# Two small copies of a state-space layer moved from compute engines to DMA, in a kernel whose instruction order is planned at build time

## The chip, the cores and the metric

The kernel runs on one core of one Trainium2 chip. The metric is the device time of one execution in microseconds (us), the median of several runs. Engine names are those of the profile: PE is TensorE's matmul, PEld its weight load, DVE is VectorE, ACT is ScalarE, POOL is GpSimd, and SP is SyncE, which in this kernel only issues DMAs.

## The reference, cut to what matters

Two layers act on `x` of shape 2 x 2048 x 256. Each layer normalises its input, computes a branch `s` and a gate `g`, and adds `s * silu(g)`. In the first layer `s` is a Mamba block and `g` an FFN with blockwise FP4 quantisation; in the second layer `s` is a small attention (its softmax runs over the batch of two) and `g` three blocks of a quantised linear pair with LoRA. The change concerns the Mamba block:

```python
xi, z = jnp.split(x @ in_proj_w, 2, axis=-1)             # 512 channels each
xc = lax.conv_general_dilated(xi, conv_w, padding=[(3, 0)], ...)   # causal, 4 taps, per channel
xc = silu(xc + conv_b)
dt, Bm, Cm = jnp.split(xc @ x_proj_w, [16, 32], axis=-1)
dt = softplus(dt @ dt_proj_w + dt_proj_b)
def step(h, inp):                                        # one time step, h: 512 channels x 16 states
    h = exp(dt_t * A) * h + dt_t * B_t * x_t
    y = sum(h * C_t, axis=-1)
    return h, y
_, ys = lax.scan(step, h0, xs)                           # 2048 steps, batch 2
y = (ys + D * xc) * silu(z);  s = y @ out_proj_w
```

Two things are carried along the sequence: the last three columns of `xi`, which the causal convolution needs, and the state `h`.

## The kernel before

**Chunks.** The sequence is cut into 8 chunks of T = 256 steps, for each of two batch rows b. The order is (j, b) with j outermost, so there are 16 chunk steps; the chunk of (j, b) needs what (j-1, b) left two steps earlier. A chunk step has four parts: `head` (normalise, in-projection, convolution, `dt`, `B`, `C`), `fp4_half`, `scan` and `tail`. After both batch rows of a j, `second` computes the second layer for two groups of 128 steps.

**The convolution.** `xi` is a tile of 128 partitions x 4 channel groups x (3 + 256) columns with one buffer. ACT fills columns 3 and on from PSUM; columns 0 to 2 are the history, from a small constant tile `hist[b]`. After ACT's copies the last three columns go back to `hist[b]`. In the kernel before both moves are DVE copies of 128 x 12 elements. PE multiplies `xi` with diagonal matrices `cdiag`, 16 products of 256 columns to a bank.

**The recurrence.** `scan` takes the 16 states in 8 pairs, so there are 128 pairs in all. For each pair: a DMA brings B and C, broadcast to all partitions, into `bcs` (two buffers); ACT writes eight pieces of `decay = exp(dt * A)`; DVE writes `ux * B` into `hh` columns 1 to 256 (call it the product with B); column 0 of each of the 8 rows of `hh`, the seed, is the carried state from `state[b]`; one DVE scan runs over all 8 rows, 2056 elements; a DMA saves the last column to `state[b]`; DVE multiplies by C, shifted one column; PE transposes 16 blocks into the accumulating banks `y`. The tile `hh` has two buffers, so the seed and the product with B of pair k need the transposes of pair k-2 done. At j = 0 the seed is a memset on POOL (16 pairs); in the other 112 pairs it is an ACT copy of 128 x 8 elements.

**The order of the work.** Nothing is issued as it is written. `Recorder` records each call, with its stage (chunk step, part); `prepare` finds what depends on what; `forward` plays the program on a small model of the engines, whose durations come from `cost`, picking at each free engine the call of highest key; `backward` does the same from the end and gives new keys. `order` alternates both, once for each entry of the list `passes` (18 of them here, with hand-set offsets for a stage, or for a stage on one engine). `issue` then emits the calls in the order found, all of them on one line, so that in the profile nearly every instruction stands at L579 and is told by its tiles. Each engine and SP's queue execute in that order; buffers of each tile are handed out by the same plan. DMAs have a cost in the model of 0.52 us on SP, a tail of 1.7 us and 165e3 bytes per us.

Of the kernel before, what the change touches and what calls it, by code (L numbers as in the profile page):

```python
# [12 lines left out]
ALU = mybir.AluOpType  # L13
# [9 lines left out]
T = 256  # L23
# [18 lines left out]
class Recorder:  # L42
# [69 lines left out]
    def cost(self, engine, method, args, kwargs):  # L112
        out = kwargs.get("out", args[0] if args else None)
        n = 1
        for d in out.shape[1:]:
            n *= d
        if engine == "sync":
            return 0.52
        if engine == "gpsimd":
            if method == "memset":  # L120
                return 0.04
            return 0.69 if method == "tensor_tensor" else 0.19
        values = list(args[1:]) + list(kwargs.values())
        tiles = [v for v in values if hasattr(v, "tensor") and v is not out]
        if engine == "tensor":
            rhs = args[2] if len(args) > 2 else kwargs.get("rhs")
            if method == "transpose" or kwargs.get("is_transpose"):
                return 0.109
            if rhs.dtype == BF16:
                return 0.005 + n / 2400.0  # L130
            lhs = kwargs.get("lhsT", args[1] if len(args) > 1 else None)
            if lhs.shape[0] == 16 and lhs.offset >= 16 * lhs.ap[0][0]:
                return 0.1
            return 0.005 + 4 * max(n, 192) / 2400.0
        scalars = 0
        for v in tiles:
            m = 1
            for d in v.shape[1:]:
                m *= d
            scalars += m == 1 and n > 1  # L140
        if engine == "scalar":
            inside = bool(tiles) and self.space(tiles[0].tensor) == PSUM
            scalars += 1.5 * (kwargs.get("accum_out") is not None)
            return (0.05 if inside else 0.093) + 0.000833 * n + 0.1 * scalars
        if method == "tensor_tensor_scan":
            return 0.068 + 0.002083 * n
        if method == "bn_stats":
            return 0.333
        if method == "bn_aggr":
            return 0.1  # L150
        if method == "reciprocal":
            return 0.06 + 0.0066 * n
        if method == "tensor_reduce":
            n = 1
            for d in args[1].shape[1:]:
                n *= d
        if method in ("tensor_copy", "tensor_scalar", "memset") and n >= 64:
            if tiles and self.space(tiles[0].tensor) == PSUM:
                return 0.067 + 0.0010417 * n + 0.06 * scalars
            return 0.07 + 0.00052 * n + 0.06 * scalars  # L160
        if n <= 32:
            return 0.078
        return 0.067 + 0.0010417 * n + (0.06 if method == "scalar_tensor_tensor" and scalars else 0.0)
# [419 lines left out]
def tile_two_layers(ctx: ExitStack, tc: tile.TileContext, a: dict):  # L583
    nc = tc.nc
    rec = Recorder(nc, ctx.enter_context(tc.tile_pool(name="shadow", bufs=1, space=DRAM)))
# [124 lines left out]
    hist = [const.tile([P, 4, 3], F32, tag=f"hist{b}", name=f"hist{b}") for b in range(B)]  # L710
# [5 lines left out]
    state = [const.tile([P, NS, 4], F32, tag=f"state{b}", name=f"state{b}") for b in range(B)]  # L716
# [184 lines left out]
    def head(b, j, xt):  # L901
        nm = f"{b}_{j}"
        xn = io.tile([P, TG, D], F32, tag="xn", name=f"xn_{nm}", bufs=2)
        xh = t2k("m", f"xh_{nm}").rearrange("p (g d) -> p g d", g=TG)


        mv = statistics("m", xt, TG, f"x{nm}")
        rr = inverse_root("m", mv[:, :, 1], TG, 1.0 + EPS, EPS * EPS, f"a{nm}", (1.0, EPS))
        rh, rx = rr[:, :TG], rr[:, TG:]
        normalize("m", xh, xt, TG, mv, rh, f"a{nm}")  # L910
        normalize("m", xn, xt, TG, mv, rx, f"x{nm}")
        pt = transpose_pair("m", xh, f"a{nm}")
        lnt = mam.tile([P, 2, T], F32, tag="lnt", name=f"lnt_{nm}")
        for c in range(2):
            rec.scalar.activation(
                lnt[:, c, :], pt[:, c, :], AF.Identity,
                bias=ln1b[:, c : c + 1], scale=ln1g[:, c : c + 1],
            )
        xi = mam.tile([P, 4, T + 3], F32, tag="xi", name=f"xi_{nm}", bufs=1)
        if j == 0:  # L920
            rec.vector.memset(xi[:, :, 0:3], 0.0)
        else:
            rec.vector.tensor_copy(xi[:, :, 0:3], hist[b])
        for pr in range(2):
            px = bank("m", f"px_{nm}_{pr}").rearrange("p (m t) -> p m t", m=2)
            for mm in range(2):
                m = 2 * pr + mm
                for c in range(2):
                    rec.tensor.matmul(
                        px[:, mm, :], lhsT=w_in[:, c, m * P : (m + 1) * P], rhs=lnt[:, c, :],  # L930
                        start=(c == 0), stop=(c == 1),
                    )
            rec.scalar.copy(xi[:, 2 * pr : 2 * pr + 2, 3:], px)
        if j < NJ - 1:
            rec.vector.tensor_copy(hist[b], xi[:, :, T : T + 3])
        xc = mam.tile([P, 4, T], F32, tag="xc", name=f"xc_{nm}", bufs=1)
        for pr in range(2):
            pc = bank("m", f"pc_{nm}_{pr}").rearrange("p (m t) -> p m t", m=2)
            for mm in range(2):
                m = 2 * pr + mm  # L940
                for k in range(4):
                    rec.tensor.matmul(
                        pc[:, mm, :], lhsT=cdiag[:, m, k, :], rhs=xi[:, m, k : k + T],
                        start=(k == 0), stop=(k == 3),
                    )
            for mm in range(2):
                m = 2 * pr + mm
                rec.scalar.activation(xc[:, m, :], pc[:, mm, :], AF.Silu, bias=conv_b[:, m : m + 1])
        pd = bank("m", f"pxp_{nm}")
        for m in range(4):  # L950
            rec.tensor.matmul(
                pd[: 4 * R, :T], lhsT=w_xp[:, m].rearrange("p a b r -> p (a b r)"), rhs=xc[:, m, :],
                start=(m == 0), stop=(m == 3),
            )
        xdbl = mam.tile([4 * R, T], F32, tag="xdbl", name=f"xdbl_{nm}", bufs=1)
        rec.scalar.copy(xdbl, pd[: 4 * R, :T])
        bc = dram.tile([2 * NS, T], F32, tag="bc", name=f"bc_{nm}")
        for q in range(2):
            rec.sync.dma_start(bc[q * NS : (q + 1) * NS, :], xdbl[(2 * q + 1) * R : (2 * q + 2) * R, :])
        dt = mam.tile([P, 4, T], F32, tag="dt", name=f"dt_{nm}")  # L960
        ux = mam.tile([P, 4, T], F32, tag="ux", name=f"ux_{nm}", bufs=1)
        pdt = [
            bank("m", f"pdt_{nm}_{pr}").rearrange("p (m t) -> p m t", m=2)[:, :, :T]
            for pr in range(2)
        ]
        for mm in range(2):
            for pr in range(2):
                rec.tensor.matmul(
                    pdt[pr][:, mm, :], lhsT=w_dt[32 * pr : 32 * pr + R, mm * P : (mm + 1) * P],
                    rhs=xdbl[32 * pr : 32 * pr + R, :], start=True, stop=True,  # L970
                )
        for m in range(4):
            rec.scalar.activation(
                dt[:, m, :], pdt[m // 2][:, m % 2, :], AF.Softplus, bias=dt_b[:, m : m + 1]
            )
        rec.vector.tensor_tensor(ux, dt, xc, ALU.mult)
        return dict(xt=xt, xn=xn, lnt=lnt, xc=xc, dt=dt, ux=ux, bc=bc)

    def scan(b, j, h):
# [11 lines left out]
        for n in range(0, NS, 2):  # L991
# [14 lines left out]
            if j == 0:  # L1006
                rec.gpsimd.memset(hh[:, :, :, 0], 0.0)
            else:
                rec.scalar.copy(hh[:, :, :, 0], state[b][:, n : n + 2, :])
            rec.vector.tensor_tensor(hh[:, :, :, 1:], un, bn, ALU.mult)  # L1010
            flat = hh.rearrange("p k m t -> p (k m t)")
            rec.vector.tensor_tensor_scan(
# [294 lines left out]
    for i, (j, b) in enumerate(order):  # L1307
# [48 lines left out]
        (80, 1, 0.1, 0.3, 0.08, [(1, 0, -0.16), (12, 4, -0.06)]),  # L1356
        (50, 0.1, 0.1, 0.2, 0.08, []),
        (30, 0.5, 0.05, 0.567, 0.05, [(0, 1, 0.179), (1, 2, 'gpsimd', 0.202), (10, 1, 'vector', 0.118), (10, 4, 0.653), (11, 4, 'tensor', -0.045), (13, 3, 'tensor', 0.2), (14, 0, -0.07), (15, 2, 'gpsimd', -0.336), (4, 4, 'vector', 0.127), (5, 0, 0.109), (8, 4, 1.201), (9, 1, 'gpsimd', -0.424)]),
        (80, 1, 0.02, 1, 0.05, []),
        (20, 1, 0.1, 2, 0.02, []),  # L1360
        (20, 0.5, 0.1, 0.5, 0.12, [(11, 3, 'tensor', 0.138), (3, 0, 'tensor', -0.771), (5, 0, 'scalar', 0.427)]),
        (80, 0.1, 0.05, 2, 0.08, []),
        (20, 1, 0.1, 0.5, 0.12, []),
    ]
    rec.issue(tc, lead=(12.22, -6.26, 0, -7.42, 1.15), bonus=193.318, ahead=0.034, adjust=adjust, passes=passes)

# [47 lines left out]
```

## Time and profile before

| | |
|---|---|
| time, median of 3 runs | 1745.32 us (1740.76 to 1745.61) |
| the profiled execution | 1740.26 us, span 1738.5 us |
| granted TensorE clock, mean | 0.962 |
| busy, share of the span: DVE | 1629.0 us, 94% |
| PE | 1554.3 us, 89% |
| ACT | 1472.7 us, 85% |
| POOL | 180.2 us, 10% |
| DMA, share of 16 engines | 21.3%, 179358 packets |

The page gives busy time for each engine, then 40 slices of the span with a digit for each (9 is 90% or more), the DMA queues, the chain of work that ended last, and the costliest groups of instructions: engine, operation, output tile `<-` input tiles, shapes, count, busy time, mean of one, and the idle time of that engine just before them with what ended it. The chain starts from the last instruction and steps back to what released each one.

Three rows bear on the change. The ACT copies of the seed are 112 of 204 ns mean, 22.8 us in all. The two DVE copies of the history are 14 each, of 155 and 164 ns, 2.2 and 2.3 us. The DMA that saves the state, 112 times 4 KB, takes 606 ns of SP to issue and lands 2.3 us after its issue (median).

### The profile page before, as it was taken

The page shows a single profiled execution, that of the slowest core. Times are in us where ns is not written, and L with a number is a line of the kernel's source. Part 1 is how long each engine was busy: PE and PEld are TensorE (multiplying, and loading weights), DVE is VectorE, ACT ScalarE, POOL GpSimd, SP SyncE. Part 2 cuts the span into 40 slices and gives each one's busy share as a digit, 9 for nine tenths or more (in the row PEclk, how much of TensorE's full clock was granted, in tenths as well). Part 3 has the DMA queues.
Part 4 walks back from the last instruction along what each step waited for, and adds up shares of the span by engine and source line. Part 5 has one row for each costly group of instructions (what it writes and reads, how often), then busy time and mean ns, then how long its engine had stood idle before and what let it go on. Part 6 is the DMA issues. An engine that isn't in the chain of part 4 may idle for free.

```text
span 1738.5 us, 22023 instructions
## 1 busy us (share of the span) xinstructions
PE 1554.3 (89%) x7948; PEld 1224.5 (70%) x7948; DVE 1629.0 (94%) x1658; ACT 1472.7 (85%) x2903; POOL 180.2 (10%) x122
## 2 busy tenths in 40 slices
PE   7546978899899999989998999999899989997996
PEld 5335757687686868678785777787676767776765
DVE  8999999999999999999999999999999999999623
ACT  6546877779899999989998989999999998999443
POOL 0000100111110111100101002110202011200000
PEclk9768989999999999999999999999999999999999
DMA  7322121212212222222222221222122121111000
GB/s 182 94 57 49 39 55 44 49 40 55 42 50 62 37 52 48 56 43 50 50 50 62 48 45 46 54 43 56 38 49 50 44 56 43 50 43 50 6 6 13
DMA packets 179467, 87.23 MB, mean 50 GB/s; under 512 B 131575, under 2 KB 145565, under 8 KB 179358
## 3 DMA queue, kind: packets, MB, share of 16 engines
q1 hardware_dynamic: 179358, 85.83, 21.3%
q8 instruction: 62, 1.02, 0.2%
q14 instruction: 47, 0.39, 0.1%
HBM read 80.62 MB, written 4.72 MB: 49 GB/s over the span
## 4 chain that ended last, share of the span: by engine, by line
PE 28%; DVE 19%; ACT 11%; issue 6%; POOL 0%; ACTq 0%; DVEq 0%
DVE hh L579 13%; PE bank_f L579 11%; PE bank_m L579 6%; PE bank_s L579 5%; PE bank_y L579 4%; ACT L579 4%; ACT decay L579 3%; ACT t2k_s L579 2%; PE bank_h L579 2%; DVE fp_l L579 2%; DVE fp_sc L579 1%; DVE t2k_s L579 1%; ACT t2k_f L579 1%; DVE h L579 1%; ACT dt L579 0%
## 5 line engine op out<-in xcount | busy, mean ns | idle before, releaser
L579 DVE TENSOR_TENSOR_SCAN hh<-decay,hh 128x2056 f32<-128x2056 f32 x128 | 567.3, 4432 | 4.0 <-ACT decay L579 1.9
L579 ACT ACT_TABLE_LOAD x364 | 467.0, 1283 | 22.0 <-DVE hh L579 8.2
L579 ACT ACTIVATE decay<-dt,amat 128x256 f32<-128x256 f32 x1024 | 443.4, 501 | 48.8 <-DVE hh L579 47.2
L579 PE MATMUL bank_y<-ident,hh 128*128 128x128 f32 x2048 | 280.3, 283 | 48.1 <-DVE hh L579 43.4
L579 PEld LDWEIGHTS bank_y<-ident,hh 128*128 128x128 f32 x2048 | 246.1, 146 | 86.8 <-issue 43.8
L579 DVE TENSOR_TENSOR hh<-ux,bcs 128x2048 f32<-128x2048 f32 x128 | 291.7, 2279 | 2.9 <-PE bank_y L579 2.7
L579 DVE TENSOR_TENSOR hh<-hh,bcs 128x2048 f32<-128x2048 f32 x128 | 292.0, 2282 | 0.4
L579 POOL TENSOR_TENSOR ln_sq_s<-ln_sq_s,power 128x2 f32<-128x2 f32 x42 | 73.1, 1741 | 713.6 <-ACT ln_sq_s L579 713.6
L579 PE MATMUL bank_f<-w_f,t2k_f 128*128 128x256 f32 x512 | 129.6, 384 | 6.8 <-ACT t2k_f L579 6.7
L579 PE MATMUL bank_f<-t2k_f,w_f 128*128 128x256 f32 x512 | 122.9, 381 | 1.4 <-ACT t2k_f L579 1.1
L579 PE MATMUL bank_m<-xi,cdiag 128*128 128x256 f32 x512 | 123.5, 379 | 0.7 <-ACT xi L579 0.7
L579 PEld LDWEIGHTS bank_f<-w_f,t2k_f 128*128 128x128 f32 x512 | 93.2, 191 | 25.5 <-ACT t2k_f L579 11.7
L579 PEld LDWEIGHTS bank_f<-t2k_f,w_f 128*128 128x128 f32 x512 | 95.3, 190 | 18.1 <-ACT t2k_f L579 3.7
L579 PEld LDWEIGHTS bank_m<-xi,cdiag 128*128 128x128 f32 x512 | 94.4, 190 | 15.5 <-ACT xi L579 1.1
L579 PE MATMUL bank_f<-w_down,hq 128*128 128x256 f32 x384 | 97.7, 393 | 4.7 <-ACT hq L579 4.6
L579 PE MATMUL bank_h<-t2k_s,w_l 128*128 128x256 f32 x360 | 88.6, 385 | 9.9 <-ACT t2k_s L579 9.9
L579 DVE SCALAR_TENSOR_TENSOR fp_l<-fp_h,fp_l 128x704 f32<-128x704 f32 (+2 forms) x124 | 91.5, 738 | 5.2 <-ACT fp_h L579 4.6
L579 PE MATMUL bank_f<-w_gate,t2k_f 128*128 128x352 f32 x256 | 91.7, 479 | 4.9 <-ACT t2k_f L579 3.1
L579 PE MATMUL bank_f<-w_up,t2k_f 128*128 128x352 f32 x256 | 90.0, 468 | 6.7 <-DVE h L579 3.7
L579 PEld LDWEIGHTS bank_f<-w_down,hq 128*128 128x128 f32 x384 | 73.3, 197 | 22.5 <-ACT hq L579 8.7
L579 PE MATMUL bank_s<-w_qkv,t2k_s 128*128 128x256 f32 (+1 forms) x280 | 83.8, 432 | 4.0 <-DVE t2k_s L579 4.0
L579 PE MATMUL bank_s<-w_l,t2k_s 128*128 128x256 f32 x336 | 82.6, 384 | 4.5 <-ACT t2k_s L579 4.5
(191 smaller groups left out, 2454.5 us busy)
## 6 DMA issues: line engine op xcount, KB each, us to landing
bcs<-bc SPq DMA_DIRECT2D x128, 512.0 KB, 4.8
xt<-in_x_dram SPq DMA_DIRECT2D x16, 256.0 KB, 3.8
out_dram<-t2k_s SPq DMA_DIRECT2D x15, 256.0 KB, 2.2
w_f<-in_ffn_w_dram SPq DMA_DIRECT2D x2, 1024.0 KB, 9.7
state<-hh SPq DMA_DIRECT2D x112, 4.0 KB, 2.3
t2k_s<-in_qweights_dram SPq DMA_DIRECT2D x6, 256.0 KB, 5.9
w_in<-in_in_proj_w_dram SPq DMA_DIRECT2D x1, 1024.0 KB, 5.4
h<-in_w_gate_dram SPq DMA_DIRECT2D x6, 128.0 KB, 2.2
```

The source lines that it names most:

```text
L579: getattr(getattr(self.nc, engine), method)(*args, **kwargs)
```

## The change

The seed of `hh` is brought by a DMA on SP's queue instead of an ACT copy; the history is written and read back by DMAs on SP's queue instead of DVE copies. In the cost model a power on POOL is priced by its number of columns and another two-operand call there at 0.5. The last five entries of `passes` are replaced by nine others, so that the order of all instructions and the buffers are found anew; the first thirteen entries, `lead`, `bonus`, `ahead` and `adjust` stay.

```diff
         if engine == "gpsimd":
             if method == "memset":
                 return 0.04
-            return 0.69 if method == "tensor_tensor" else 0.19
+            if args[-1] == ALU.pow:
+                return 0.39 + 0.155 * n
+            return 0.5 if method == "tensor_tensor" else 0.19
...
-            rec.vector.tensor_copy(xi[:, :, 0:3], hist[b])
+            rec.sync.dma_start(xi[:, :, 0:3], hist[b])
...
-            rec.vector.tensor_copy(hist[b], xi[:, :, T : T + 3])
+            rec.sync.dma_start(hist[b], xi[:, :, T : T + 3])
...
-                rec.scalar.copy(hh[:, :, :, 0], state[b][:, n : n + 2, :])
+                rec.sync.dma_start(hh[:, :, :, 0], state[b][:, n : n + 2, :])
...
-        (80, 1, 0.02, 1, 0.05, []),
-        (20, 1, 0.1, 2, 0.02, []),
-        (20, 0.5, 0.1, 0.5, 0.12, [(11, 3, 'tensor', 0.138), (3, 0, 'tensor', -0.771), (5, 0, 'scalar', 0.427)]),
-        (80, 0.1, 0.05, 2, 0.08, []),
-        (20, 1, 0.1, 0.5, 0.12, []),
+        (110, 1, 0.02, 0.5, 0.05, [(11, 0, 0.05), (8, 2, -0.05)]),
+        (50, 0.3, 0.02, 1, 0.08, [(0, 4, -0.29)]),
+        (110, 0.3, 0.02, 0.2, 0.05, []),
+        (20, 1, 0.1, 1, 0.08, [(3, 0, -0.05)]),
+        (50, 1, 0.02, 2, 0.12, [(0, 2, -0.2)]),
+        (80, 0.5, 0.0, 0.2, 0.02, []),
+        (80, 0.5, 0.02, 0.3, 0.05, [(9, 0, 0.1)]),
+        (110, 1, 0.0, 0.2, 0.08, [(2, 2, 0.02)]),
+        (20, 0.1, 0.1, 0.5, 0.05, [(11, 2, 'gpsimd', 1.321), (13, 3, 'vector', -0.068), (8, 0, 'gpsimd', -0.605)]),
```

Counted from the two programs: DMAs on SP go from 381 to 521 (112 seeds, 14 histories out and 14 in); ACT's copies from 350 to 238 and its table loads from 364 to 351; DVE's copies from 37 to 9. Instructions that only wait go from 55 to 142 on PE, from 350 to 372 on DVE, from 272 to 367 on SP and from 331 to 266 on ACT. Every other kind of instruction has the same count.

## The prediction

> **What bounds the kernel now.** I read the page first (busy shares, slices), then stretches of the span, then who waits for whom on DVE, then the timeline around single pairs and the chain of waits near the end. The page:
>
> ```profile
> DVE  8999999999999999999999999999999999999623
> ACT  6546877779899999989998989999999998999443
> ```
>
> The stretches (columns after the length: PE, PEld, DVE, ACT, POOL busy, then clock, DMA share, GB/s):
>
> ```profile
> 200.00:400.00 200.00, 173.15 (x868) 136.56 (x867) 197.98 (x177) 157.54 (x300) 16.45 (x9) 0.94 0.21 48
> ...
> 1000.00:1200.00 200.00, 192.96 (x1014) 155.77 (x1012) 196.49 (x191) 187.96 (x369) 22.99 (x13) 0.99 0.21 46
> 1200.00:1400.00 200.00, 186.08 (x978) 146.50 (x978) 192.89 (x181) 190.33 (x373) 26.00 (x13) 1.00 0.22 49
> ...
> 1600.00:1671.00 71.00, 66.49 (x312) 51.89 (x310) 37.42 (x53) 39.28 (x83) 3.31 (x4) 0.95 0.05 11
> 1671.00:1738.40 67.40, 50.64 (x222) 37.55 (x222) 27.09 (x76) 22.59 (x40) 5.59 (x8) 0.91 0.04 12
> ```
>
> From 200 to 1600 us the seven stretches hold 1375.2 us of DVE in 1400: 24.8 us of idle time there, and 10.6 before 200. PE and ACT follow at 93 to 96%, so DVE sets the pace, with little room under either neighbour. After the last scan (it ends at 1613.7) DVE is mostly idle: to 1671 PE is at 94% and the chain of waits runs almost wholly through it; after that come the dependent steps of the second layer. Three limits, then: DVE's sum to about 1600, PE's queue to 1671, a chain to the end.
>
> What DVE waits for from 200 to 1600 (us in total, times, longest):
>
> ```profile
> DVE t2k_s L579 <- PE bank_s L579: 4.6, 4, 2.4
> DVE hh L579 <- PE bank_y L579: 2.7, 3, 1.6
> ...
> DVE hh L579 <- ACT decay L579: 1.9, 2, 1.2
> ```
>
> No wait is large. Little is to be won in this stretch, much could be lost.
>
> **The change part by part.** Durations are from the profiled execution, which took 1740.26 us (span 1738.5, 1.8 outside it). It stands 5.1 under the median of 1745.32 and at the lower end of the runs.
>
> *DVE copies.* 28 go, 155 and 164 ns, together 4.5 us. They overlap their neighbours: the one at 28.18 us of the timeline is followed by the next DVE start at 28.26, 0.08 us on, so 2.2 to 4.5; I take 3, on the saturated engine.
>
> *ACT copies and table loads.*
>
> ```profile
> L579 ACT COPY hh<-state 128x8 f32<-128x8 f32 x112 | 22.8, 204 | 7.4 <-PE bank_y L579 5.6 <-DVE hh L579 1.8
> L579 ACT ACT_TABLE_LOAD x364 | 467.0, 1283 | 22.0 <-DVE hh L579 8.2 <-PE bank_f L579 3.8 <-PE bank_h L579 1.7
> ```
>
> 112 copies give 22.8 us back, and ACT no longer stands in its queue for the transposes (5.6). The new order has 13 table loads fewer, 13 x 1.283 = 16.7. The Trainium skill (ScalarE: Activation LUTs, What ACT_TABLE_LOAD costs) prices a switch at 2.66 us, since a drain of 1.38 comes with the load; that would be 34.6. The trace shows no such drain: a load from 1590.46 for 1.28 us is followed by its ACTIVATE at 1591.76. So 16.7, and 39.5 in all. This lies beside DVE: ACT feeds it late only for a few us. What a lighter ACT can bring is a part of the 24.8 us of DVE idle, directly or through PE, which waits for ACT in turn; bounds 0 and 15, I take 5 (about the waits on ACT and POOL plus a share of those on PE).
>
> *The seed as a DMA.* No row shows a DMA into `hh`; the nearest is the same 1024 elements the other way:
>
> ```profile
> bcs<-bc SPq DMA_DIRECT2D x128, 512.0 KB, 4.8
> ...
> state<-hh SPq DMA_DIRECT2D x112, 4.0 KB, 2.3
> ```
>
> The skill speaks against this (DMA: Bandwidth & Descriptors, Rules for kernel authors): under 64 KB one pays mostly overhead, and a strided last dimension costs a descriptor for each element, as here, against a copy of 0.2 us. Taken on the path, 112 x 2.3 = 258 us. But the same table says to issue early and wait late, and the trace decides by the room there is. The seed may start when the transposes of pair k-2 end and must be there when scan k starts. A tight case:
>
> ```profile
> 1188.55 0.27 PE L579 MATMUL bank_y<-ident,hh 128*128 128x128 f32 x1
> 1188.86 2.29 DVE L579 TENSOR_TENSOR hh<-ux,bcs 128x2048 f32<-128x2048 f32 x1 [0.47 <-PE bank_y L579]
> 1190.82 0.20 ACT L579 COPY hh<-state 128x8 f32<-128x8 f32 x1
> 1191.26 4.44 DVE L579 TENSOR_TENSOR_SCAN hh<-decay,hh 128x2056 f32<-128x2056 f32 x1
> ```
>
> The last transpose ends at 1188.82, the scan starts at 1191.26: 2.4 us, because DVE does its product first. The same difference over all 112 pairs has a median of 8.2 us; 10 are below 3.0, 12 below 4, 25 below 5, 35 below 5.8. A seed that needs 2.9 (0.6 of issue, 2.3; counting the issue twice at worst) would lack 2.6 us in total in the old order, one that needs 4 would lack 14. SP's queue adds its own order. In the new program I traced, for each seed, what SP must have seen before it gets there: always the transposes of k-2 (once k-3), and a DVE instruction after which DVE still has, at the rows' durations, 11.9 us of work (median) before the scan; the smallest is 2.2, the next 3.5. `bcs`, queued behind seeds that wait for PE, keeps at least 4.6 (median 10.6) against 4.8 + 0.4 needed, because what blocks it is usually the transposes of the pair three before. So +1 us, bounds 0 and 14.
>
> *The histories.* 28 DMAs; the first convolution product waits for one. `xi<-hist` starts when the previous convolution frees `xi`, and the in-projection (8 products of 0.43) and ACT's `xi` copies (0.59) come in the same interval. The cover is the eight scans of the current chunk, some 95 us, beside which the next `head` runs. 0; if the cover were gone, 14 x 2.9 = 41 for PE, of which DVE would see what it waits for at `ux`.
>
> *SP, PE and DVE's waits.* SP issues 112 x 0.61 + 28 x about 0.5 = 82 us more; it waits 747 us for DVE's `hh` today. PE gets 87 more waiting instructions; at the 0.04 us that the chain shows as "issue" between dependent steps that is 3.5 us on an engine with 7 us free in each 100. DVE gets 22: +0.9 by the same price.
>
> *The end.* Behind the transposes of pair 124 the old order leaves PE 148 products of 128 columns, 179 of 256, 16 of 352 and 21 of 512; the new one 152, 179, 16 and 21. DVE has 133 and 135 instructions left behind scan 124, ACT 23 and 21 table loads. So from about 1590 us both have the same work, and all that differs before must come out of DVE's stretch. +0.5; bounds -3 and +5 for the inner order.
>
> Sum: -3 - 5 + 1 + 0.9 + 0.5 = -5.6, so 1734.7 for an execution like the profiled one. The median before stood 5.1 above its profiled run; since I don't know whether this repeats, I add 1.3 of it and say 1736.
>
> **The rivals.**
> *A, the forecast (0.57)*: DVE's sum shrinks, its idle time too. 1722 to 1743.
> *B, nothing comes out of it (0.18)*: DVE's idle time stays at some 25 us, since waits on PE make most of it and PE's work is the same (1554 us busy). Then -3 + 1 + 0.9 + 0.5, about -1: 1740 to 1748. For it: ACT's direct share of the waits is a few us. Against it: ACT is the one engine that gets 39 us free.
> *C, the seed comes late (0.17)*: on the rings it follows a 512 KB `bcs` transfer, directly in 62 of 112 cases, and lands with it, 4.8 us or more after issue. Place: between the product with B and the scan; the scan then stalls DVE, and behind it stand the multiply by C, the FP4 work and the next product, for which PE's transposes wait. At 5.8 us from the transposes the shortages of the old order add up to 56 us; half of it (62 of 112) is 28, less the 9 won: about 1762. It decides from a landing at which the shortages reach 9 us, about 3.5 us after the transposes. For it: 512 KB at 4.8 us is the largest thing on the rings. Against it: the median of 11.9 us in the queue.
> *D, the new order loses in the end phase (0.08)*: a convolution late, or the FFN of the last chunk pushed behind second-layer work; 5 to 15 us, about 1755.
>
> **How the numbers follow.** 0.3% (5.2 us) is about what a measurement of this kernel can tell from no change. Faster means below 1740.1: nearly all of A, a little of B, 0.56. Same, 1740.1 to 1750.6: most of B, the edge of A, 0.19. Slower: C, D, 0.25. The range reaches from A's best (15 of idle time gone: 1724, less the lower bounds) to the nearer part of C: 1720 to 1757. Within A alone it is 1722 to 1743.
>
> **What would show it.** Right: DVE busy near 1625 with `hist` and `xi<-hist` gone from its rows, DVE idle of 16 to 22 us in 200 to 1600, ACT busy near 1433 with 351 table loads, `hh<-state` on SP landing in about 2.3 us, the last scan ending near 1607. Wrong by C: a row "DVE hh <- DMA hh<-state" of over 9 us. Wrong by D: the last scan earlier, the end later. Also wrong if DVE's waits on PE grow past 20 us in the scan stretch though no DMA is late.

## The result, and the profile after

The changed kernel takes 1761.94 us (median of 4 runs, 1758.53 to 1765.93) against 1744.16 us before (4 runs, the three shown above and one more). The ratio is 1.0106, with a 95% interval of 1.0077 to 1.0134: slower, by 18.5 us (0.0106 times 1743; the medians are 17.8 apart). The forecast was 1736 us, faster, with a range that ended at 1757. The profiled execution took 1763.68 us, span 1761.9, at a mean granted clock of 0.954 (0.962 before). The two traces are 23.4 us apart in span, more than the 18.5, so a shift read from one to the other is somewhat too large. Within one kernel the time goes with this clock: of the 27 runs of the kernel before that were taken beside experiments 1 to 4, the ten at 0.952 to 0.957 took 1748.1 to 1752.7 us, the five at 0.965 and 0.966 took 1738.3 to 1738.7. The four runs of the changed kernel, at 0.954 to 0.957, lie above all of these. So the clock does not make the loss, but it can hold a part of it, and no run here shows which of the two follows the other.

Every line number is two higher (L581 for L579). The page of the changed kernel, busy time and the slices of DVE and ACT:

```profile
PE 1567.4 (89%) x7948; PEld 1236.2 (70%) x7948; DVE 1617.2 (92%) x1630; ACT 1444.6 (82%) x2778; POOL 168.1 (10%) x122
...
DVE  7899999999999999999998999989999999999623
ACT  5645867879999898999988999889999889989443
```

Both engines are busy for less time, as was meant: DVE 11.8 us less, ACT 28.1 less. But DVE's row, nines from the second slice to the end of the scans before, now has two eights in the middle. The same stretches as before (PE, PEld, DVE, ACT, POOL busy, then clock, DMA share, GB/s), and one from the end of the last scan:

```profile
200.00:400.00 200.00, 174.63 (x878) 135.41 (x877) 199.00 (x192) 152.61 (x285) 9.33 (x9) 0.95 0.26 51
1000.00:1200.00 200.00, 192.80 (x1010) 153.21 (x1009) 192.04 (x172) 181.33 (x349) 19.39 (x11) 0.99 0.28 48
1200.00:1400.00 200.00, 192.33 (x990) 151.60 (x989) 191.01 (x188) 195.25 (x371) 25.03 (x14) 0.99 0.27 50
1400.00:1600.00 200.00, 187.89 (x972) 147.08 (x971) 190.06 (x166) 173.90 (x346) 27.68 (x12) 0.98 0.22 46
1633.00:1762.00 129.00, 108.09 (x491) 81.64 (x489) 51.61 (x125) 54.61 (x107) 8.34 (x12) 0.95 0.03 9
```

At 200 to 400 us DVE is fuller than before (199.0 for 198.0); from 1000 on it stands idle for 8 to 10 us in each 200, at nearly the same clock. Over 200 to 1600 us its idle time goes from 24.8 to 48.3 us, and before 200 us from 10.6 to 18.7. The last scan ends at 1633.2 us, 19.5 later than before; what follows it takes 128.7 us for 124.8.

Was it a late DMA? The rows of the seed, with the rows of the scan and of the convolution:

```profile
L581 DVE TENSOR_TENSOR_SCAN hh<-decay,hh 128x2056 f32<-128x2056 f32 x128 | 567.1, 4431 | 5.5 <-DMA hh<-state 2.2
L581 ACT ACT_TABLE_LOAD x351 | 450.3, 1283 | 24.0 <-PE bank_h L581 7.5
...
L581 PE MATMUL bank_m<-xi,cdiag 128*128 128x256 f32 x512 | 125.1, 382 | 0.0
...
state<-hh SPq DMA_DIRECT2D x112, 4.0 KB, 2.3
hh<-state SPq DMA_DIRECT2D x112, 4.0 KB, 3.2
```

All scans together lose 2.2 us to seeds (4 times), though a seed lands 3.2 us after its issue (median) and not 2.3, as the DMA that saves the state does. The convolutions' row (`bank_m<-xi,cdiag`) has 0.0 us of idle time before it, so no history was late either. What DVE waits for from 200 to 1600 us:

```profile
DVE hh L581 <- PE bank_y L581: 8.1, 5, 3.0
DVE h L581 <- PE bank_f L581: 6.0, 8, 1.4
DVE ux L581 <- ACT dt L581: 4.5, 2, 3.7
...
DVE hh L581 <- DMA hh<-state: 2.2, 4, 0.9
```

All of DVE's rows that name PE add up to 20.9 us (11.5 before), those that name ACT to 19.9 (4.8 before). So PE and ACT come late, though PE has the same products to do and ACT less than before. One step further back, ACT's own waits in that stretch, first before, then after:

```profile
ACT t2k_s L579 <- POOL ln_sq_s L579: 0.7, 1, 0.7
```

```profile
ACT t2k_s L581 <- POOL ln_sq_s L581: 15.4, 8, 4.4
```

This is the largest change of any of ACT's rows, and it belongs to work that the change does not touch. In the second layer ACT accumulates squares into `ln_sq_s` (128 x 2), POOL raises these two columns to the power -0.5, and ACT scales with the result (42 times in all). The longest case in the timeline (start, length, engine, and in brackets the idle time before and what ended it):

```profile
1397.31 0.29 ACT L581 ACTIVATE ln_sq_s<-ln_sq_s,eps 128x2 f32<-128x2 f32 x1
...
1397.67 6.73 POOL L581 TENSOR_TENSOR ln_sq_s<-ln_sq_s,power 128x2 f32<-128x2 f32 x1 [30.21 <-ACT ln_sq_s L581]
...
1399.48 4.43 DVE L581 TENSOR_TENSOR_SCAN hh<-decay,hh 128x2056 f32<-128x2056 f32 x1
...
1404.44 0.84 ACT L581 ACTIVATE t2k_s<-bank_s,ln_sq_s 128x256 f32<-128x256 f32 x2 [4.44 <-POOL ln_sq_s L581]
...
1405.33 0.87 PE L581 MATMUL bank_s<-ident,t2k_s 128*128 128x128 f32 x4 [4.03 <-ACT t2k_s L581]
...
1406.88 2.29 DVE L581 TENSOR_TENSOR hh<-ux,bcs 128x2048 f32<-128x2048 f32 x1 [2.96 <-PE bank_y L581]
```

A power on two columns takes 6.73 us: it starts while DVE is in a product, DVE goes on through an FP4 step and a scan without a gap, and the power ends half a microsecond after the scan does. ACT stands behind it for 4.44 us, PE behind ACT for 4.03, and the transposes that free `hh` stand behind that in PE's queue, so DVE loses 2.96. At 930.80 us (4.88 long, behind a product and shorter steps) and 1142.89 us (4.96, behind a scan) the same happens, with 3.7 us lost on DVE in one gap and 4.0 in three.

The powers are hardly slower than before. POOL's row for them, before and after (count | busy, mean ns | idle before):

```profile
L579 POOL TENSOR_TENSOR ln_sq_s<-ln_sq_s,power 128x2 f32<-128x2 f32 x42 | 73.1, 1741 | 713.6 <-ACT ln_sq_s L579 713.6
```

```profile
L581 POOL TENSOR_TENSOR ln_sq_s<-ln_sq_s,power 128x2 f32<-128x2 f32 x42 | 77.5, 1844 | 756.8 <-ACT ln_sq_s L581 756.8
```

Of all two-column powers on POOL, 7 in each kernel run beside 4 us or more of a scan; these took 4.5 to 5.6 us before and 4.8 to 6.7 after, and 25 and 33 of the other 73 took 0.70 to 0.75. What differs is which of them end later than the plan had them; the plans are set beside the traces after experiments 3 and 4.

### The profile page after: what moved, and what is told of

It reads as the page before. It is cut to its first block, busy times and chain, and to the rows that moved or that the text cites. A ratio compares the mean times of both kernels' runs of the same rounds, so it can differ in the third digit from the quotient of the medians.

```text
span 1761.9 us, 22149 instructions
## 1 busy us (share of the span) xinstructions
PE 1567.4 (89%) x7948; PEld 1236.2 (70%) x7948; DVE 1617.2 (92%) x1630; ACT 1444.6 (82%) x2778; POOL 168.1 (10%) x122
## 5 line engine op out<-in xcount | busy, mean ns | idle before, releaser
L581 DVE TENSOR_TENSOR_SCAN hh<-decay,hh 128x2056 f32<-128x2056 f32 x128 | 567.1, 4431 | 5.5 <-DMA hh<-state 2.2
L581 ACT ACT_TABLE_LOAD x351 | 450.3, 1283 | 24.0 <-PE bank_h L581 7.5
L581 ACT ACTIVATE decay<-dt,amat 128x256 f32<-128x256 f32 x1024 | 440.4, 500 | 34.8 <-DVE hh L581 26.1
L581 PE MATMUL bank_y<-ident,hh 128*128 128x128 f32 x2048 | 281.2, 282 | 41.3 <-DVE hh L581 41.3
L581 PEld LDWEIGHTS bank_y<-ident,hh 128*128 128x128 f32 x2048 | 245.5, 146 | 79.2 <-issue 45.1
L581 DVE TENSOR_TENSOR hh<-ux,bcs 128x2048 f32<-128x2048 f32 x128 | 291.6, 2279 | 9.4 <-PE bank_y L581 8.1
L581 DVE TENSOR_TENSOR hh<-hh,bcs 128x2048 f32<-128x2048 f32 x128 | 291.5, 2278 | 0.1
L581 POOL TENSOR_TENSOR ln_sq_s<-ln_sq_s,power 128x2 f32<-128x2 f32 x42 | 77.5, 1844 | 756.8 <-ACT ln_sq_s L581 756.8
L581 PE MATMUL bank_f<-w_f,t2k_f 128*128 128x256 f32 x512 | 132.0, 389 | 10.7 <-ACT t2k_f L581 10.5
L581 PE MATMUL bank_f<-t2k_f,w_f 128*128 128x256 f32 x512 | 125.2, 385 | 3.5 <-ACT t2k_f L581 2.0
L581 PE MATMUL bank_m<-xi,cdiag 128*128 128x256 f32 x512 | 125.1, 382 | 0.0
L581 PEld LDWEIGHTS bank_f<-w_f,t2k_f 128*128 128x128 f32 x512 | 94.7, 193 | 31.2 <-ACT t2k_f L581 18.3
L581 PEld LDWEIGHTS bank_f<-t2k_f,w_f 128*128 128x128 f32 x512 | 96.6, 192 | 22.0 <-ACT t2k_f L581 4.7
L581 PE MATMUL bank_h<-t2k_s,w_l 128*128 128x256 f32 x360 | 93.9, 400 | 14.2 <-ACT t2k_s L581 14.1
L581 PEld LDWEIGHTS bank_m<-xi,cdiag 128*128 128x128 f32 x512 | 95.1, 192 | 13.9 <-issue 0.2
L581 DVE SCALAR_TENSOR_TENSOR fp_l<-fp_h,fp_l 128x704 f32<-128x704 f32 (+2 forms) x124 | 91.6, 739 | 11.7 <-ACT fp_h L581 11.4
L581 PE MATMUL bank_f<-w_down,hq 128*128 128x256 f32 x384 | 99.3, 402 | 3.2 <-ACT hq L581 3.1
L581 PE MATMUL bank_f<-w_gate,t2k_f 128*128 128x352 f32 x256 | 91.1, 476 | 2.9 <-ACT t2k_f L581 1.4
L581 PE MATMUL bank_f<-w_up,t2k_f 128*128 128x352 f32 x256 | 89.8, 471 | 2.4 <-ACT sg L581 1.9
L581 PEld LDWEIGHTS bank_h<-t2k_s,w_l 128*128 128x128 f32 x360 | 66.4, 197 | 33.3 <-ACT t2k_s L581 23.1
L581 PEld LDWEIGHTS bank_f<-w_down,hq 128*128 128x128 f32 x384 | 75.3, 201 | 20.5 <-ACT hq L581 7.1
L581 PE MATMUL bank_f<-ident,fp_l 128*128 128x128 f32 x292 | 50.9, 303 | 39.8 <-DVE fp_l L581 32.4
```

The costliest lines, as they stand in the source:

```text
L581: getattr(getattr(self.nc, engine), method)(*args, **kwargs)
```

## The experiments

The order of the calls can be kept fixed while a call goes to another engine, is left out, or moves, since the order is a list that `issue` walks. "The order of before" and "the changed order" mean this list. Ratios are to the kernel before, run on the same chip at the same time.

**1. The changed order, with the copies back.**

```diff
+                if i in self.seeds:      engine, method = "scalar", "copy"
+                if i in self.histories:  engine, method = "vector", "tensor_copy"
                 getattr(getattr(self.nc, engine), method)(*args, **kwargs)
```

> The order of the changed kernel, call for call, but the 112 seeds are again ACT copies and the 28 histories DVE copies, each at the place in the order where the plan had put the DMA. Theory ORDER (the order found anew is what costs, the DMAs themselves are hidden): 1758 to 1772, since the 18 us stay and 22.8 us of ACT and 3 of DVE come back. Theory DMA (seeds or histories land late, or the waits on them hold up PE): the time falls to about 1745 to 1750.

1768.45 us (1764.6 to 1770.59), ratio 1.0129 [1.0104, 1.0155]. The loss stays without a single seed or history DMA, so it comes from the order. The same row stands in this trace: ACT waits 11.9 us for POOL's powers (7 times). Whether the DMAs are better than the copies in this order is not clear: the ratios give 4 us (1.0129 less 1.0106, times 1743), within their intervals.

**2. The order of before, with the DMAs**, each moved on SP's queue to right behind the last call that it waits for.

```diff
+        order = self.early(order, self.seeds | self.histories)   # only these 140 calls move
...
+                if i in self.seeds or i in self.histories:  engine, method = "sync", "dma_start"
```

> The order of the kernel before, call for call, but with the DMAs of the change, each moved forward in the order to right behind the last call that it has to wait for (for a seed the transposes of pair k-2). Theory ORDER: 1734 to 1746, a small gain from 3 us of DVE and 22.8 us of ACT. Theory DMA: 1755 to 1765 as in the changed kernel.

1749.08 us (1744.38 to 1754.27), ratio 1.0025 [1.0011, 1.004]. DVE's waits in this kernel:

```profile
DVE hh L607 <- DMA hh<-state: 6.2, 7, 1.5
DVE hh L607 <- PE bank_y L607: 5.0, 4, 2.4
```

This lies between the ranges of the two theories. In an order not made for them the DMAs cost some 4 us, inside the bounds of 0 and 14 that the prediction had for late seeds, and far from 18.5.

**3. Before, with the new price and passes, and 4. the changed calls with the old price and passes.**

```diff
 # 3: rec.scalar.copy / rec.vector.tensor_copy as before; new price in cost(), new entries of passes
 # 4: rec.sync.dma_start as after; old price in cost(), old entries of passes
```

> Copies as before, but the new list of passes and the new price of POOL calls in the cost model, so the order is found anew without any DMA. Theory ORDER, if the list makes poor orders: 1752 to 1768. Theory DMA: 1740 to 1750. A value in between would say that each list fits one kernel by chance.

> The DMAs of the change with the old list of passes and the old price of POOL calls: a third order. Theory ORDER, if it is the new list that is poor: 1735 to 1748. Theory DMA: 1755 to 1765. If orders scatter by themselves whatever list is used: anything from 1735 to 1775.

1793.62 us (1793.02 to 1794.42), ratio 1.0277 [1.025, 1.0304], and 1768.53 us (1765.88 to 1773.69), ratio 1.0139 [1.011, 1.0167]. The first is above every range that was expected for it; the second is above those of both theories and inside the one for orders that scatter. Neither part of the edit can be judged alone this way, since a list of passes is fitted to one set of calls. The planner itself says so. The end of its last `forward` is a plan, no time of the chip; beside the measured spans:

| | planned end | span | span less plan |
|---|---|---|---|
| before | 1734.4 | 1738.5 | 4.1 |
| 3: copies, new list | 1785.7 | 1791.8 | 6.1 |
| 4: DMAs, old list | 1760.4 | 1765.8 | 5.4 |
| after | 1734.2 | 1761.9 | 27.7 |

Three orders run 4 to 6 us past their plan. The changed one was planned to end with the old one and runs 27.7 past: something that the plan does not hold strikes this order far more than the others. Taking the planned start of each scan from its measured start (both counted from the first scan), the changed kernel slips by 29.8 us up to the last scan and the old one by 9.6. Its three largest steps, 4.8, 3.8 and 3.1 us, are at the scans that start at 1171.6, 943.1 and 1411.3 us, soon behind the three powers above.

The planner does know that DVE holds POOL up. In `forward` of both kernels (cut; `table[i]` is 1 for every POOL call but a memset):

```python
if best_e == "gpsimd" and table[i]:
    t = max(t, free["vector"])
```

A power starts in the plan only when DVE's call in progress has ended. What the plan does not hold is a power that has to wait for the DVE call after that as well. Counted from the end of the ACT instruction before it, in the trace and in the plan, all 42 powers of the old order end at most 0.8 us later than planned, the longest (4.55 us) too. In the changed order 38 do so, and four end 3.2 to 4.9 us later than planned: those that start at 732.72, 930.80, 1142.89 and 1397.67 us. ACT's scaling starts 0.03 or 0.04 us after each of these four has ended, and they make 12.6 of the 15.4 us that ACT waits for POOL. The distance that was planned from a power's end to its reader on ACT is no shorter in the changed order: 0.7 us (median), against 0.6.

**5. The powers left out**, in both orders.

```diff
-                rec.scalar.activation(sq, sq, AF.Identity, scale=1.0 / D, bias=eps)
+                rec.scalar.activation(sq, sq, AF.Identity, scale=0.0, bias=eps)
...
+                if i in self.powers:  continue      # POOL's 42 powers on ln_sq_s
```

> The changed kernel, its order call for call, but POOL's 42 powers of the second layer (ln_sq_s, between ACT's accumulated squares and ACT's scaling) are left out, and the tile they would have raised is a constant. Theory P: in the changed order ACT comes to 8 of these powers while POOL is still held up by DVE's scans (15.4 us of ACT waiting on POOL against 0.7 before), PE then waits for ACT, and DVE for PE; without the powers 11 to 17 us come back, 1745 to 1751. Rival S: the new order is worse in many places that have nothing to do with POOL; then at most the last 3 us come back, 1758 to 1763.

> The kernel before with the same 42 powers left out, the tile again a constant. In its order ACT waits once for such a power, 0.7 us. Theory P and rival S both say 1741 to 1745; P fails as an explanation of the difference if this kernel gains as much as the changed one does.

In the changed order: 1750.08 us (1747.51 to 1751.59), ratio 1.0044 [1.0031, 1.0057]. In the order of before: 1742.12 us (1737.71 to 1743.98), ratio 0.9997 [0.9988, 1.0005]. The same 42 instructions cost nothing in one order and about 10.8 us in the other (1.0106 less 1.0044, times 1743; by the two intervals give or take some 5). The slip of the last scan from the plan falls from 29.8 to 16.7 us, against 12.5 in the order of before without the powers. The last scan, first in the changed order and then in that of before, both without powers (start, length):

```profile
1615.02 4.44 DVE L584 TENSOR_TENSOR_SCAN hh<-decay,hh 128x2056 f32<-128x2056 f32 x1
```

```profile
1614.16 4.44 DVE L582 TENSOR_TENSOR_SCAN hh<-decay,hh 128x2056 f32<-128x2056 f32 x1
```

Up to there the two orders are now level, 0.9 us apart, where it was 19.5.

**6. The power replaced by a memset on POOL**, in the changed order: the way from ACT to POOL and back stays, with its semaphores.

```diff
+                if i in self.powers:  method, args = "memset", [args[0], 0.5]
```

> The changed kernel, its order call for call; each of the second layer's 42 powers on POOL is a memset of the same two columns on POOL instead, so that the way ACT, POOL, ACT with its semaphores stays and only the power itself is left out (the columns become a constant). POOL's memsets of hh took 0.11 to 0.12 us in every trace, beside scans or not, where the powers took 0.70 to 6.7. Theory P (it is the power's stretching by DVE's work that costs the 11.9 us): 1748 to 1753, as with the powers left out, and ACT's wait on POOL under 3 us. Rival H (the hop over POOL itself, or the power's planned 0.7 us, is too much for an order without slack): over 1756.

1748.49 us (1744.16 to 1753.4), ratio 1.0032 [1.0021, 1.0042].

```profile
L584 POOL MEMSET ln_sq_s<- 128x2 f32 x42 | 4.2, 99 | 781.7 <-ACT ln_sq_s L584 781.7
```

```profile
ACT t2k_s L584 <- POOL ln_sq_s L584: 0.4, 2, 0.2
```

So it is neither the hop over POOL nor its queue, but the power's own time, and 12.9 us come back (1.0106 less 1.0032, times 1743; again give or take some 5). The memset takes 99 ns on average in the same places where the power took 1844; nine of the 42 lie wholly inside a scan and took no longer. The Trainium skill (SBUF — State Buffer, Who interferes with whom, with the blocking also in Summary: rules for kernel authors) has the rule that fits both rows: a DVE instruction with two SBUF inputs contends with a GpSimd instruction that reads SBUF, not with one that only writes, and the one that comes second is blocked for the whole instruction. The scans and products here have two SBUF inputs; the power reads and is stretched from 0.70 to 4.4 us and more, the memset only writes and is not. In the trace of before a power that starts 0.05 us into a scan takes 4.88 us and one that starts 3.43 us into a scan takes 1.44: both end some 0.5 us after that scan. That it is the port was not tried by itself; that the power is stretched beside DVE and a writing instruction is not, these rows show. Of the powers on two columns that begin during a DVE instruction and take over 0.76 us, 48 of 52 in the trace of before and 41 of 47 in that of after end some 0.5 us after that instruction, most of them though the next one follows without a gap. Why the four late ones had to wait for further instructions too stays open.

**7. The power kept, its followers moved back.** Whatever hangs on a power is set back in the queues by as much as it would be late if each power took 4.4 (or 2.2) us longer than planned.

```diff
+        order = self.late(order, 4.4)    # at[i] = max(start[i], at[p] + cost[p] + delay (+ 4.4 if p is a power))
```

> The changed kernel with all of its work; its order is kept, except that whatever hangs on one of the 42 powers of the second layer on POOL is moved back in the queues by as much as it would be late if each power took 4.4 us longer than planned (one scan on DVE); what has slack stays where it was, what doesn't hang on them too. Theory P: ACT's 15.4 us of waiting on POOL fall below 4, DVE's idle time with them, and most of the 11.9 us come back that leaving the powers out gave: 1749 to 1755. Rival Q: the wait is only moved, since PE and ACT then reach the second layer's steps later and the tail grows by it: 1758 to 1763.

> The same with 2.2 us instead of 4.4. Theory P: the powers that a whole scan holds up are still too late by some 2 us each, so about half comes back: 1752 to 1758. Rival Q: 1758 to 1763.

1780.04 us (1778.21 to 1780.78), ratio 1.0206 [1.0191, 1.0222], and 1768.54 us (1766.75 to 1771.27), ratio 1.0143 [1.0126, 1.016]. My expectation failed: ACT's wait on POOL fell to 4.2 and 7.9 us, yet both kernels are slower than the changed one. In the first the last scan ends 7.0 us later, and what follows it takes 137.7 us for 128.7; in the second 1.7 and 3.5 us are added. So less waiting on POOL did not bring a shorter time here. The followers of all 42 powers were set back, though only four come late; where the added time arises was not taken apart. The cause stands on experiments 5 and 6; a mend was not found.

**8. Which DMA costs what, in the order of before.** The histories alone, the seeds alone (both moved as in 2), and all of them at the very places of the copies.

```diff
 # histories alone: order = self.early(order, self.histories);  seeds alone: self.early(order, self.seeds)
 # all in place: no early(), only engine and method change
```

> The order of the kernel before, call for call, the seeds still ACT copies, only the 28 history copies are DMAs, each moved on SP's queue to right behind the last call it waits for. If the histories are hidden behind the scans, as the prediction had it, DVE loses 28 copies (4.5 us of durations, 3 on the path) and nothing waits: 1740 to 1742. If the earlier 5 us of loss with all 140 DMAs in this order come from the histories, 1748.

> The order of the kernel before, call for call, the histories still DVE copies, only the 112 seeds are DMAs, each moved on SP's queue to right behind the last call it waits for. With all 140 DMAs in this order DVE waited 6.2 us for seeds. If those are the cost, 1748 to 1752; if not, 1743 to 1745.

> The order of the kernel before, call for call, with all 112 seeds and 28 histories as DMAs at the very places where the copies stood, so that nothing is issued early. If a DMA's landing (2.3 us, 0.6 of issue) then stands on the path of many scans, the row of DVE's hh waiting for hh<-state holds most of the difference: with a median of some 1 us for each of 112 pairs about 100 us, 1800 to 1870. If the copies' places are early enough, 1747 to 1755 as with the DMAs moved forward (1749 in its session).

Histories: 1744.93 us (1740.97 to 1754.32), ratio 1.0033 [1.0017, 1.005]. Seeds: 1745.41 us (1742.1 to 1749.92), ratio 1.0021 [1.0012, 1.0031]. All in place: 1763.59 us (1759.95 to 1763.89), ratio 1.0109 [1.0094, 1.0124]. In the last one:

```profile
DVE hh L584 <- DMA hh<-state: 15.9, 9, 3.8
```

The seeds behave as the prediction had it: issued where the copies stood, 9 of them are late and DVE waits 15.9 us; issued early it waits 5.5 with the seeds alone and 6.2 with all DMAs, and with an order that knows of them 2.2. The time with the seeds alone lies between the two that were expected. I had expected either some 100 us or 5 for all in place; it is 19.5. The histories are a miss, and the time lies in neither range. In the trace nothing waits for them, but the 28 DVE copies bring nothing back: DVE's busy time falls by 0.6 us (1629.0 to 1628.4), not by 4.5, and two traces with the same DVE instructions differ as much (1629.0, and 1629.8 without the powers). In the changed order the same copies are worth 3.3 us of DVE's busy time (1620.5 with them in experiment 1, 1617.2 without). Five of the 15 runs with the histories alone took over 1752 us, where none of the 33 of the kernel before beside them took over 1745.4; the trace is of a run of 1743.69. Why is open.

## Why the prediction was wrong

**What held.** DVE sets the pace to about 1600 us. ACT lost 112 copies and 13 table loads (351 of 1283 ns), without a drain of its own per switch; its busy time fell by 28.1 us rather than 39.5, since copies overlap their neighbours (with the copies back in the same order it is 10.2 higher, not 22.8). DVE's busy time is 1617 us for the 1625 forecast, but 8.5 of the 11.8 us come from the order alone (1620.5 with the copies back), which the sum did not have. The seeds cost 2.2 us where the sum had +1 (bounds 0 and 14); they land 3.2 us (median) after their issue, not the 2.3 that was taken from the DMA the other way, and there was room for it. Rival C fell: DVE's wait for seeds is 2.2 us, not the over 9 that it named, with the 512 KB `bcs` transfers on the same queue. The histories have their cover. The end phase took 3.9 us more, inside the bounds of -3 and +5.

**The step that failed** is the term "lighter ACT": -5, with bounds of 0 and 15, on DVE's idle time of 24.8 us. It treated the order found anew as something that can only use the room that a lighter ACT gives, and had no side for a loss. I compared the two orders by amounts (instructions behind pair 124, waiting instructions, SP's places) and did not ask which calls of another engine might come later than the new plan has them. In the trace the idle time went to 48.3 us, a loss of 23.5 where a gain of 5 was written down. The powers are some 11 to 13 us of the time, and four of them are what came late. The gain itself is not seen either: without the powers DVE idles 36.0 us from 200 to 1600 in the changed order and 26.7 in the old one.

**What was in view.** The trace of before showed the stretched power: its row has a mean of 1741 ns, while the shortest of the 42 took 0.70 us. I read POOL as 10% busy and passed on, and ACT's wait of 0.7 us as nothing to lose. That row itself was no sign, since the plan had reckoned with all of its stretching. The sign was in the first layer: its powers at 179.12 and 569.70 us took 5.55 and 5.35 us, through the rest of a short DVE step and then a whole scan, which is longer than one DVE call can hold them. Neither the plan nor the new price in `cost` has this: a two-column power gets 0.39 + 0.155 x 2 = 0.70 us, the time of one that DVE leaves alone, behind the one DVE call in progress. Which powers of the new order it would strike could not be read from the old trace.

**The last line of the prediction**, "also wrong if DVE's waits on PE grow past 20 us in the scan stretch though no DMA is late", is what happened: 20.9 us. No chance had been set on it; it should have been a rival with a price, and rival D put the danger of a new order into the end phase only.

**What is left.** Without the powers' stretching the changed kernel is still 6 to 8 us slower than before. A part of this goes with the clock: at 0.959 to 0.962 the ten runs of experiment 6 average 1746.8 us and the 15 of the kernel before beside them 1743.4. In the traces without powers the tail after the last scan takes 128.8 us against 122.3, at a granted clock of 0.95 there against 0.99; in the trace of before it took 124.8 at 0.95. PE has the same products in both kernels and is busy for 108.0 of the 128.8 us: DVE and ACT work that is saved earlier does not shorten that. No experiment here takes the tail apart, so this is read, not shown. No version that was run beats the kernel before.

## What to carry to other kernels

When a planner makes an order anew, its loss or gain is a term of its own with both signs, and the amount of work in each engine does not give it. Set the trace beside the plan, call by call: a row whose mean is far above its shortest instance stood in both traces here, and what told the two orders apart is the four calls that ended later than planned. An engine that is 10% busy can still set the time where another one stands right behind such a call. To find such a cause, keep the order and leave out the one suspected instruction in both kernels: it is dear in one and free in the other.

## What the runs showed of the hardware

- A POOL power that reads two columns took 0.70 to 0.75 us in 25 and 33 of 80 cases (before and after), and 4.5 to 6.7 us beside 4 us or more of a scan of 4.43 us. Of those that fall into a DVE instruction, 48 of 52 and 41 of 47 end some 0.5 us after it, mostly though the next one follows without a gap; the others, four of them the late ones of the changed order, wait for further instructions. A memset of a few columns on POOL took 0.10 to 0.12 us, beside a scan too.
- A 4 KB DMA of 1024 four-byte elements within SBUF takes 0.6 us of SP to issue; those that save the state land 2.3 us after it (median), those that bring the seed 3.2 (longest 6.6). 112 more of them leave DVE's and ACT's instruction times unchanged (scan 4431 ns, table load 1283 ns).
- Taking 28 copies of 155 and 164 ns off a DVE that is 94% busy lowered its busy time by 0.6 us in one order and by 3.3 in the other.
